# A step's x taken one step later in VectorE's order; the gate's moments on VectorE alone; the weights summed from x's place

## The chip, the cores and the metric

The kernel runs on one core of one Trainium2 chip. The metric is the device time of one execution in microseconds (us), as the median of timed runs. One more execution was taken with the hardware profiler on; the profile and the trace come from that one. The five engines of the core are called TensorE (PE in the profile; PEld is its weight load), VectorE (DVE), ScalarE (ACT), GpSimd (POOL) and SyncE (SP).

## The reference, cut to what matters

It is the forward pass of a recommender with attention over a user's history. The batch is B = 16,384, the history L = 200 items long, an embedding D = 64 numbers in float32, the item table 100,000 rows. In short:

```python
def dice(x, alpha, axis):
    mean = jnp.mean(x, axis=axis, keepdims=True)
    var = jnp.var(x, axis=axis, keepdims=True)
    p = jax.nn.sigmoid((x - mean) * jax.lax.rsqrt(var + EPS))
    return x * (p + alpha * (1.0 - p))

u, it, c = u_emb[user], i_emb[item], c_emb[cate]
h = i_emb[hist]                                   # [L, B, D]
itb = jnp.broadcast_to(it[None], h.shape)
feat = jnp.concatenate([h, itb, h - itb, h * itb], axis=-1)
a = dice(feat @ au_W1 + au_b1, au_alpha, axis=1)  # [L, B, 36]: moments over the batch
w = a @ au_W2 + au_b2                             # [L, B, 1]
cur = jnp.sum(w * h, axis=0)                      # [B, D]
z = jnp.concatenate([u, it, c, cur], axis=-1)
z = dice(z @ W1 + b1, alpha1, axis=0)
z = dice(z @ W2 + b2, alpha2, axis=0)
return z @ W3 + b3
```

The expensive part is the attention: 200 x 16,384 rows are looked up, each goes through a layer of 36 outputs, and the gate of that layer needs mean and variance over the whole batch of one history place before it can be applied.

## The kernel before

**Setup.** The layer is split by linearity. What depends on h alone (h times the first and third block of au_W1) is put behind each row of the item table once, so that `table` in DRAM has 128 numbers a row: h, and its part of x. What depends on the item alone is stored as `xi`. What is left for each history place is the product of h * item with the fourth block (`blk_m`).

**Steps.** A step k handles one chunk of 2,048 batch rows (16 rows on each of 128 partitions) of one history place: l, c = divmod(k, 8), so that eight steps make a place and 1,600 steps the whole. Seven turns of a hardware loop hold 24 places each (192 steps); the last 32 places (256 steps, `K`) follow without a loop, with pieces of the head's first layer (`base_of_layer1`, through `next(work)`) between them. At every loop turn all engines meet. The order of the instructions on each engine is the order of the program text (`manual_schedule`). Step k works on several chunks at once:

- `fetch(k)`: POOL issues sixteen indirect gathers of 128 rows each (L212) from `table` into one of twelve landing buffers `land`; SP loads `xi` of the chunk into one of two `xit` buffers.
- `gates(k-10)`: on ACT, sigmoid with scale and bias (L404, two halves) from x, which lies in the second half of the landing buffer's rows, into `pg` in PSUM, and then the line with alpha and the second layer's weight (L409). The scale and bias of a place are known only when its eight chunks have been through `hidden`, hence the distance of ten steps.
- `hidden(k-2)`: VectorE adds the product in PSUM (`px`) and the turned x part (`hx[:, 1]`), writes x into the landing buffer (L396), and takes batch statistics of both halves (L398).
- ACT copies `xit` into `px` (L482), onto which the product is accumulated.
- `turn(k-1)`: VectorE transposes h (L389) into `ph`, multiplies with the item (L390), and transposes the x part (L391). L389 is the first to need the gathered rows.
- `gated(k-10)`: VectorE multiplies gate and x (L415).
- `first_layer(k-1)`: TensorE's product, four matmuls of 128 x 512 in float32, each recorded as two (L243).
- `weigh(k-10)`: VectorE transposes the gated values (L420) into `hx[:, 0]`, sums 64 numbers for each row (L422), multiplies the row h with that weight (L427, scalar_tensor_tensor of `r` and `land`, both in SBUF), and adds to `cur` (L431).

`px` has two buffers that take turns in the loop; in the last 256 steps only the first is used for it, since the second (`pz`) takes the head's pieces.

**The end of a place.** In the step in which `hidden` handles the eighth chunk (`ends`), `bn_aggr` gives mean and variance of each partition (L438); the four groups of 32 partitions have to be averaged. That goes over TensorE: a matmul with the constant matrix `mean_of[S]` for the mean (L442), squares of deviations on VectorE (L447 to L449), a second matmul for the variance (L450), Sqrt on ACT (L452, with a table load[...]), and reciprocal and shift on VectorE (L458, L459). These pieces are laid between `turn`, `gated`, `first_layer` and `weigh`.

Of the kernel before, what the change touches and what calls it, by code (L numbers as in the profile page):

```python
# [14 lines left out]
P = 128  # L15
D = 64
# [5 lines left out]
LAND = 12  # L22
EARLY = 4
# [5 lines left out]
def din_kernel(  # L29
# [86 lines left out]
    for a in range(P // S):  # L116
# [19 lines left out]
    rstds = [const.tile([P, 2], F32, name=f"rs{i}") for i in range(2)]  # L136
    shifts = [const.tile([P, 2], F32, name=f"sh{i}") for i in range(2)]
# [27 lines left out]
        n: const.tile([n * m, n * m], F32, name=f"mean{n}") for n, m in ((ZA, 2), (ZB, 2 * J), (Z2, 2), (S, P // S))  # L165
# [182 lines left out]
    with ExitStack() as main:  # L348
# [20 lines left out]
        for i in range(2):  # L369
            nc.vector.memset(rstds[i], 0.0)  # L370
            nc.vector.memset(shifts[i], 0.0)
        nc.sync.dma_start(xit[-1 % XI], xi[ND - 1])

# [3 lines left out]
        def x_of(k):  # L377
            return land[k % LAND][:, :, D:]

# [13 lines left out]
        def hidden(k, px):  # L393

            l, c = divmod(k, ND)
            nc.vector.tensor_add(x_of(k), by_row(px), by_row(hx[k % 2][:, 1]))  # L396
            for q in range(2):
                nc.vector.bn_stats(stats[l % 2][:, q, c, :], x_of(k)[:, ts(q, TD // 2)])  # L398

        def gates(k):  # L400

            i = k // ND % 2
            for q in range(2):
                nc.scalar.activation(  # L404
                    by_row(pg)[:, ts(q, TD // 2)], x_of(k)[:, ts(q, TD // 2)], AF.Sigmoid,
                    bias=shifts[i][:, q : q + 1], scale=rstds[i][:, q : q + 1],
                )
# [6 lines left out]
        def gated(k):  # L414
            nc.vector.tensor_mul(by_row(pg), by_row(pg), x_of(k))  # L415

        def weigh(k):

            yT = hx[k % 2][:, 0]
            nc.vector.transpose(yT, pg)  # L420
            r = small.tile([P, TD], F32, tag="r", name="r")
            nc.vector.tensor_reduce(  # L422
                r, halves(yT).rearrange("p q n u -> p n q u"), mybir.AxisListType.XY, ALU.add
# [9 lines left out]
        mean, var = ph[:, 0:2], ph[:, 8:10]  # L433

        def moments_by_row(l):
# [3 lines left out]
            return mv  # L439

        def mean_of_groups(mv):
            nc.tensor.matmul(mean, mean_of[S], mv[:, :, 0], start=True, stop=True)  # L442

        def var_of_groups(mv):

            dev = small.tile([P, 2], F32, tag="dev", name="dev")
            nc.vector.tensor_sub(dev, mv[:, :, 0], mean)  # L447
            nc.vector.tensor_mul(dev, dev, dev)
            nc.vector.tensor_add(dev, dev, mv[:, :, 1])  # L449
            nc.tensor.matmul(var, mean_of[S], dev, start=True, stop=True)  # L450
            std = small.tile([P, 2], F32, tag="std2", name="std2")
            nc.scalar.activation(std, var, AF.Sqrt, bias=eps)  # L452
            return std

        def factors(l, std):

            i = l % 2
            nc.vector.reciprocal(rstds[i], std)  # L458
            nc.vector.scalar_tensor_tensor(shifts[i], mean, -1.0, rstds[i], ALU.mult, ALU.mult)  # L459

        def step(k, last=None):
# [4 lines left out]

            def px_of(j):

                return pxs[j % 2 if last is None or j < 0 else 0]

            l, c = divmod(k - 2, ND)
            ends = has(k - 2) and c == ND - 1
            if has(k):
                fetch(k)
            if has(k - 10):
                gates(k - 10)
            if has(k - 2):
                hidden(k - 2, px_of(k - 2))
            if ends:
                mv = moments_by_row(l)  # L480
            if has(k - 1):
                nc.scalar.copy(px_of(k - 1), xit[(k - 1) % XI])  # L482
                turn(k - 1)
            if ends:
                mean_of_groups(mv)
            if has(k - 10):
                gated(k - 10)
            if ends:
# [208 lines left out]
```

## Time and profile before

| | |
|---|---|
| timed runs (3) | 32,810.53 us median, 32,810.52 to 32,812.21 |
| the profiled execution | 36,985.32 us |
| its span, first to last instruction | 36,983.5 us |
| mean granted TensorE clock in it | 0.618 |
| busy in the span | PE 27%, PEld 11%, DVE 54%, ACT 19%, POOL 68% |
| gathers from `table` | 25,600, busy 24,929.8 us, 974 ns in the mean, 945 ns in the median |
| first and last gather start | 606.1 us, 36,780.7 us |
| VectorE's idle time before L396 | 15,628.3 us |
| VectorE's idle time before L389 | 478.4 us |
| DMA | 73 GB/s in the mean, 2,682 MB |

How to read the groups of the profile: line, engine, operation, output<-inputs by the program's names, shapes and count; then after the first bar busy time in us and the mean length of one in ns; after the second bar the idle time of the engine just before these instructions, and what ended most of it. "remote" and "issue" are waits for which the profile names no instruction. The ends of matmuls are modelled, so a wait for TensorE is read at the engine that waits. A line of the timeline holds start and length in us, engine, line, operation, names, shape and count, and in brackets the idle time before it and its releaser.

The profiled execution is 4.2 ms longer than the timed ones.

### The profile page before, as it was taken

What the parts mean: (1) busy time and instruction counts of PE and PEld (TensorE: products, weight loads), DVE (VectorE), ACT (ScalarE), POOL (GpSimd) and SP (SyncE); (2) the same over time, 40 slices, a digit from 0 to 9 for tenths busy, and PEclk for the clock granted to TensorE, in tenths of its full rate; (3) what the DMA queues carried; (4) which work ended last, traced back from release to release, by engine and by line L of the source; (5) the groups of instructions that cost most, each with busy time, mean ns of one, the idle gap of its engine ahead of it and who ended that gap; (6) DMA issues with size and microseconds to landing.
All of it is one profiled execution on the core that took longest, in us unless ns stands there. A gap on an engine that the chain in (4) does not pass through costs nothing. (4 is left out here: it accounts for less than half of the span.)

```text
span 36983.5 us, 116856 instructions
## 1 busy us (share of the span) xinstructions
PE 10134.8 (27%) x14456; PEld 4044.4 (11%) x14456; DVE 20049.6 (54%) x19476; ACT 7101.7 (19%) x8732; POOL 25299.4 (68%) x25992
## 2 busy tenths in 40 slices
PE   4222222222222222222222222222222222322223
PEld 1111111111111111111111111111111111111111
DVE  4555555555555555555555555555555555555555
ACT  0111211121111111111111111111111111211122
POOL 6766676676667666666766676676666676666665
PEclk7666666666666666666666666666666666666666
DMA  4222222222222222222222222222222222222222
GB/s 142 70 70 69 72 70 70 68 73 70 69 70 72 70 70 70 70 70 70 71 70 70 71 70 69 70 72 70 70 69 70 71 70 74 82 80 76 69 70 61
DMA packets 1219253, 2682.27 MB, mean 73 GB/s; under 512 B 552540, under 2 KB 578684, under 8 KB 1212284
## 3 DMA queue, kind: packets, MB, share of 16 engines
q0 software_dynamic: 831488, 1691.97, 17.4%
q1 hardware_dynamic: 375228, 914.56, 8.1%
q10 hardware_dynamic: 11712, 67.98, 0.5%
q14 instruction: 702, 5.75, 0.1%
q8 instruction: 123, 2.02, 0.0%
HBM read 2599.36 MB, written 73.35 MB: 72 GB/s over the span
## 5 line engine op out<-in xcount | busy, mean ns | idle before, releaser
L212 POOL DMA_INDIRECT land<-table,idx x25600 | 24929.8, 974 | 11288.1 <-issue 11053.1
L243 PE MATMUL px<-hx,blk_m 128*128 128x512 f32 x12824 | 9461.7, 906 | 22646.0 <-DVE hx L390 15979.1
L396 DVE TENSOR_TENSOR land<-px,hx 128x1024 f32<-128x1024 f32 x1602 | 1959.1, 1223 | 15628.3 <-remote 13918.8
L404 ACT ACTIVATE pg<-land,sh,rs 128x512 f32<-128x512 f32 x3220 | 2515.7, 781 | 23511.4 <-issue 21445.8
L243 PEld LDWEIGHTS px<-hx,blk_m 128*128 128x128 f32 x12824 | 3683.8, 302 | 28262.8 <-issue 27321.7
L409 ACT ACTIVATE pg<-pg,au_al,au_1al 128x512 f32<-128x512 f32 x3220 | 2419.0, 751 | 106.9
L389 DVE STREAM_TRANSPOSE ph<-land 128x1024 f32<-128x1024 f32 x1601 | 1992.7, 1245 | 478.4 <-DMA land<-table,idx 474.6
L427 DVE SCALAR_TENSOR_TENSOR pg<-r,au_bias,land 128x1024 f32<-128x1024 f32 x1610 | 2084.3, 1295 | 56.7
L398 DVE BATCH_NORM_STATS2 st<-land 128x6 f32<-128x512 f32 x3204 | 2061.2, 685 | 55.1
L420 DVE STREAM_TRANSPOSE hx<-pg 128x1024 f32<-128x1024 f32 x1610 | 2009.5, 1248 | 48.9
L482 ACT COPY px<-xit 128x1024 f32<-128x1024 f32 x1601 | 1613.1, 1008 | 2124.1 <-issue 1385.9
L431 DVE TENSOR_TENSOR cur<-pg,cur 128x1024 f32<-128x1024 f32 x1610 | 1970.6, 1224 | 54.9
L422 DVE TENSOR_REDUCE r<-hx 128x16 f32<-128x1024 f32 x1610 | 1964.0, 1220 | 55.3
L390 DVE TENSOR_TENSOR hx<-ph,itT 128x1024 f32<-128x1024 f32 x1601 | 1959.5, 1224 | 54.7
L391 DVE STREAM_TRANSPOSE hx<-land 128x1024 f32<-128x1024 f32 x1601 | 1974.6, 1233 | 0.0
L415 DVE TENSOR_TENSOR pg<-pg,land 128x1024 f32<-128x1024 f32 x1610 | 1930.8, 1199 | 5.4 <-ACT pg L409 5.3
L442 PE MATMUL ph<-mv,mean 128*128 128x2 f32 x402 | 117.9, 363 | 3346.9 <-issue 1834.8
L452 ACT ACTIVATE std<-ph,eps 128x2 f32<-128x2 f32 x201 | 52.7, 262 | 2829.2 <-remote 2360.5
L442 PEld LDWEIGHTS ph<-mv,mean 128*128 128x128 f32 x402 | 100.6, 311 | 3518.0 <-issue 1928.2
L404 ACT ACT_TABLE_LOAD x209 | 268.1, 1283 | 932.9 <-DMA table<-tab 338.0
L243 PE MATMUL px<-rT,blk_h 128*128 128x512 f32 (+1 forms) x392 | 236.1, 764 | 237.6 <-DVE rT L294 124.7
L452 ACT ACT_TABLE_LOAD x201 | 257.9, 1283 | 3.5
(109 smaller groups left out, 1711.6 us busy)
## 6 DMA issues: line engine op xcount, KB each, us to landing
xit<-xi SPq DMA_DIRECT2D x1601, 512.0 KB
land<-table,idx POOLq DMA_INDIRECT x25600
table<-tab ACTq DMA_DIRECT2D x48, 1024.0 KB
tab<-in_L_rec_i_emb SPq DMA_DIRECT2D x48, 512.0 KB
zt<-uicT SPq DMA_DIRECT2D x48, 512.0 KB
idx<-in_r_hist SPq DMA_DIRECT2D x200, 64.0 KB
uicT<-t ACTq DMA_DIRECT2D x24, 512.0 KB
zbase<-zt SPq DMA_DIRECT2D x10, 512.0 KB
```

The costliest lines, as they stand in the source:

```text
L212: nc.gpsimd.indirect_dma_start(out=dst[:, n, :], out_offset=None, in_=rows, in_offset=bass.IndirectOffsetOnAxis(ap=ids[:, n : n + 1], axis=0),
L243: nc.tensor.matmul(dst[:, q * CH : q * CH + n], blk[:, e, q], rhs[:, e * CH : e * CH + n], start=(e == 0 and not onto), stop=(e == 1), ski ...
L389: nc.vector.transpose(halves(ph), of_rows(rows[:, :, :D]))
L390: nc.vector.tensor_mul(hm, ph, itT[:, k % ND])
L391: nc.vector.transpose(halves(hw), of_rows(rows[:, :, D:]))
L398: nc.vector.bn_stats(stats[l % 2][:, q, c, :], x_of(k)[:, ts(q, TD // 2)])
L404: nc.scalar.activation(by_row(pg)[:, ts(q, TD // 2)], x_of(k)[:, ts(q, TD // 2)], AF.Sigmoid, bias=shifts[i][:, q : q + 1], scale=rstds[i] ...
L409: nc.scalar.activation(pg[:, ts(q, CH)], pg[:, ts(q, CH)], AF.Identity, bias=au_al[:, q : q + 1], scale=au_1al[:, q : q + 1],)
L420: nc.vector.transpose(yT, pg)
L422: nc.vector.tensor_reduce(r, halves(yT).rearrange("p q n u -> p n q u"), mybir.AxisListType.XY, ALU.add)
L427: nc.vector.scalar_tensor_tensor(by_row(pg), r.unsqueeze(2).to_broadcast([P, TD, D]), au_bias2, rows, ALU.add, ALU.mult,)
L431: nc.vector.tensor_add(cur[:, ts(c, TD)], by_row(pg), cur[:, ts(c, TD)])
```

## The change

- In step k, `turn(k-1)` and its product come first, then the moments where a place has ended, then `gates(k-10)` and `weigh(k-10)`, then `hidden(k-2)`, and last the copy of `xit` for step k itself (`preload(k)`), so that the product of step k+1 finds it there. Only in the last 144 steps (`SPAN`), where `px` has one buffer, do copy and product come behind `hidden(k-2)`.
- `moments(l)` replaces the four pieces at the end of a place. It is called once, in the step after the eighth chunk's `hidden`, and brings the four groups together by copies between partitions and by sums on VectorE; ACT still takes the square root. Scale and bias lie together in `facs`, which is copied back to the other three groups. `mean_of[S]` is no longer made.
- `gated` becomes the first instruction of `weigh`. x is now kept in the landing buffer in the layout of the turned values; `weigh` transposes the gated values into x's place, and the sum runs over 64 numbers that lie next to each other.
- The head's pieces are called from step K - 143 on.

```diff
@@ -20,6 +20,7 @@
 CD = 2 * CH
 LPB = 24
 LAND = 12
+SPAN = 144
 EARLY = 4
 IDX = 2
 XI = 2
@@ -133,8 +134,8 @@
     stats = [
         const.tile([P, 2, ND, nc.vector.BN_STATS_DIM], F32, name=f"st{i}") for i in range(2)
     ]
-    rstds = [const.tile([P, 2], F32, name=f"rs{i}") for i in range(2)]
-    shifts = [const.tile([P, 2], F32, name=f"sh{i}") for i in range(2)]
+
+    facs = [const.tile([P, 2, 2], F32, name=f"fac{i}") for i in range(2)]
     pxs = [psum.tile([P, CD], F32, name=f"px{i}") for i in range(2)]
     px, pz = pxs
     ph = psum.tile([P, CD], F32, name="ph")
@@ -162,7 +163,7 @@
     bias3 = const.tile([S, ZO], F32, name="bias3")
 
     mean_of = {
-        n: const.tile([n * m, n * m], F32, name=f"mean{n}") for n, m in ((ZA, 2), (ZB, 2 * J), (Z2, 2), (S, P // S))
+        n: const.tile([n * m, n * m], F32, name=f"mean{n}") for n, m in ((ZA, 2), (ZB, 2 * J), (Z2, 2))
     }
     zstats = [
         const.tile([n, m, nc.vector.BN_STATS_DIM], F32, name=f"zst{i}")
@@ -367,15 +368,15 @@
             for c in range(ND):
                 nc.vector.bn_stats(stats[-1 % 2][:, q, c, :], hx[0][:, 0, :CH])
         for i in range(2):
-            nc.vector.memset(rstds[i], 0.0)
-            nc.vector.memset(shifts[i], 0.0)
+            nc.vector.memset(facs[i], 0.0)
         nc.sync.dma_start(xit[-1 % XI], xi[ND - 1])
+        nc.scalar.copy(pxs[-1 % 2], xit[-1 % XI])
 
         def by_row(t):
             return t.rearrange("p (n d) -> p n d", d=D)
 
         def x_of(k):
-            return land[k % LAND][:, :, D:]
+            return of_rows(land[k % LAND][:, :, D:])
 
         def fetch(k):
             l, c = divmod(k, ND)
@@ -393,17 +394,17 @@
         def hidden(k, px):
 
             l, c = divmod(k, ND)
-            nc.vector.tensor_add(x_of(k), by_row(px), by_row(hx[k % 2][:, 1]))
+            nc.vector.tensor_add(x_of(k), halves(px), halves(hx[k % 2][:, 1]))
             for q in range(2):
-                nc.vector.bn_stats(stats[l % 2][:, q, c, :], x_of(k)[:, ts(q, TD // 2)])
+                nc.vector.bn_stats(stats[l % 2][:, q, c, :], x_of(k)[:, q])
 
         def gates(k):
 
             i = k // ND % 2
             for q in range(2):
                 nc.scalar.activation(
-                    by_row(pg)[:, ts(q, TD // 2)], x_of(k)[:, ts(q, TD // 2)], AF.Sigmoid,
-                    bias=shifts[i][:, q : q + 1], scale=rstds[i][:, q : q + 1],
+                    halves(pg)[:, q], x_of(k)[:, q], AF.Sigmoid,
+                    bias=facs[i][:, 1, q : q + 1], scale=facs[i][:, 0, q : q + 1],
                 )
             for q in range(2):
                 nc.scalar.activation(
@@ -411,16 +412,13 @@
                     bias=au_al[:, q : q + 1], scale=au_1al[:, q : q + 1],
                 )
 
-        def gated(k):
-            nc.vector.tensor_mul(by_row(pg), by_row(pg), x_of(k))
-
         def weigh(k):
 
-            yT = hx[k % 2][:, 0]
-            nc.vector.transpose(yT, pg)
+            nc.vector.tensor_mul(halves(pg), halves(pg), x_of(k))
+            nc.vector.transpose(x_of(k), halves(pg))
             r = small.tile([P, TD], F32, tag="r", name="r")
             nc.vector.tensor_reduce(
-                r, halves(yT).rearrange("p q n u -> p n q u"), mybir.AxisListType.XY, ALU.add
+                r, land[k % LAND][:, :, D:], mybir.AxisListType.X, ALU.add
             )
             c = k % ND
             rows = land[k % LAND][:, :, :D]
@@ -430,33 +428,36 @@
             )
             nc.vector.tensor_add(cur[:, ts(c, TD)], by_row(pg), cur[:, ts(c, TD)])
 
-        mean, var = ph[:, 0:2], ph[:, 8:10]
-
-        def moments_by_row(l):
+        def moments(l):
+
+            n = P // S
             mv = small.tile([P, 2, 2], F32, tag="mv", name="mv")
             for q in range(2):
                 nc.vector.bn_aggr(mv[:, q], stats[l % 2][:, q].rearrange("p c s -> p (c s)"))
-            return mv
-
-        def mean_of_groups(mv):
-            nc.tensor.matmul(mean, mean_of[S], mv[:, :, 0], start=True, stop=True)
-
-        def var_of_groups(mv):
-
-            dev = small.tile([P, 2], F32, tag="dev", name="dev")
-            nc.vector.tensor_sub(dev, mv[:, :, 0], mean)
+            every = small.tile([S, n, 2, 2], F32, tag="every", name="every")
+            for a in range(n):
+                nc.vector.tensor_copy(every[:, a], mv[ts(a, S)])
+            means = every[:, :, :, 0]
+            mean = small.tile([S, 2], F32, tag="mean", name="mean")
+            nc.vector.tensor_reduce(
+                mean, means.rearrange("p a q -> p q a"), mybir.AxisListType.X, ALU.add
+            )
+            nc.vector.tensor_scalar_mul(mean, mean, -1.0 / n)
+            dev = small.tile([S, n, 2], F32, tag="dev", name="dev")
+            nc.vector.tensor_add(dev, means, mean.unsqueeze(1).to_broadcast([S, n, 2]))
             nc.vector.tensor_mul(dev, dev, dev)
-            nc.vector.tensor_add(dev, dev, mv[:, :, 1])
-            nc.tensor.matmul(var, mean_of[S], dev, start=True, stop=True)
-            std = small.tile([P, 2], F32, tag="std2", name="std2")
-            nc.scalar.activation(std, var, AF.Sqrt, bias=eps)
-            return std
-
-        def factors(l, std):
-
-            i = l % 2
-            nc.vector.reciprocal(rstds[i], std)
-            nc.vector.scalar_tensor_tensor(shifts[i], mean, -1.0, rstds[i], ALU.mult, ALU.mult)
+            nc.vector.tensor_add(dev, dev, every[:, :, :, 1])
+            var = small.tile([S, 2], F32, tag="var", name="var")
+            nc.vector.tensor_reduce(
+                var, dev.rearrange("p a q -> p q a"), mybir.AxisListType.X, ALU.add
+            )
+            std = small.tile([S, 2], F32, tag="std2", name="std2")
+            nc.scalar.activation(std, var, AF.Sqrt, bias=eps[:S], scale=1.0 / n)
+            fac = facs[l % 2]
+            nc.vector.reciprocal(fac[:S, 0], std)
+            nc.vector.tensor_mul(fac[:S, 1], mean, fac[:S, 0])
+            for a in range(1, n):
+                nc.vector.tensor_copy(fac[ts(a, S)], fac[:S])
 
         def step(k, last=None):
 
@@ -464,35 +465,37 @@
             def has(j):
                 return last is None or j <= last
 
+            def single(j):
+
+                return last is not None and j > last - SPAN
+
             def px_of(j):
-
-                return pxs[j % 2 if last is None or j < 0 else 0]
-
-            l, c = divmod(k - 2, ND)
-            ends = has(k - 2) and c == ND - 1
+                return pxs[0 if single(j) else j % 2]
+
+            def preload(j):
+                nc.scalar.copy(px_of(j), xit[j % XI])
+
+            def product(j):
+                first_layer(px_of(j), blk_m, hx[j % 2][:, 0], onto=True)
+
             if has(k):
                 fetch(k)
+            if has(k - 1):
+                turn(k - 1)
+                if not single(k - 1):
+                    product(k - 1)
             if has(k - 10):
+                if k % ND == 2:
+                    moments((k - 10) // ND)
                 gates(k - 10)
+                weigh(k - 10)
             if has(k - 2):
                 hidden(k - 2, px_of(k - 2))
-            if ends:
-                mv = moments_by_row(l)
-            if has(k - 1):
-                nc.scalar.copy(px_of(k - 1), xit[(k - 1) % XI])
-                turn(k - 1)
-            if ends:
-                mean_of_groups(mv)
-            if has(k - 10):
-                gated(k - 10)
-            if ends:
-                std = var_of_groups(mv)
-            if has(k - 1):
-                first_layer(px_of(k - 1), blk_m, hx[(k - 1) % 2][:, 0], onto=True)
-            if has(k - 10):
-                weigh(k - 10)
-            if ends:
-                factors(l, std)
+            if has(k - 1) and single(k - 1):
+                preload(k - 1)
+                product(k - 1)
+            if has(k) and not single(k):
+                preload(k)
 
         def fetch_ids(k, l0, n):
             l, c = divmod(k, ND)
@@ -601,7 +604,7 @@
             for k in range(K):
                 fetch_ids(k, L - rest_l, rest_l)
                 step(k, last=K - 1)
-                if k > 1:
+                if k > K - SPAN:
                     next(work, None)
             load_base(0, 1)
             for k in range(K, K + 10):

```

## The prediction

> **What bounds the kernel now.** I read four views in this order: the page's groups, who waited for whom, the timeline of one quiet step, and the timeline around a long gather. First two groups of the page with two more of VectorE's, then a line of the gathers' own view, then one of the waits:
>
> ```profile
> L212 POOL DMA_INDIRECT land<-table,idx x25600 | 24929.8, 974 | 11288.1 <-issue 11053.1
> L243 PE MATMUL px<-hx,blk_m 128*128 128x512 f32 x12824 | 9461.7, 906 | 22646.0 <-DVE hx L390 15979.1
> L396 DVE TENSOR_TENSOR land<-px,hx 128x1024 f32<-128x1024 f32 x1602 | 1959.1, 1223 | 15628.3 <-remote 13918.8
> L389 DVE STREAM_TRANSPOSE ph<-land 128x1024 f32<-128x1024 f32 x1601 | 1992.7, 1245 | 478.4 <-DMA land<-table,idx 474.6
> ...
> L212 POOL DMA_INDIRECT land<-table,idx x25600: 938/945/2163, 606.1 to 36780.7; - x199
> ...
> DVE land L396 <- remote: 13918.8, 1227, 21.2
> ```
>
> GpSimd (POOL) issues 25,600 gathers of 128 rows, sixteen to a step, 1,600 steps. The first begins at 606.1 us, the last ends at 36,781.7, and 201.8 us follow. In the profiled execution VectorE stands 15.6 ms ahead of L396 (`hidden`), which waits for TensorE. Taken alone, that line says TensorE bounds the kernel and the change goes to the right place. It has to be held against a step in which this wait does not occur (columns: start, length, engine, line; idle time in brackets):
>
> ```profile
> 6394.33 0.94 POOL L212 DMA_INDIRECT land<-table,idx  x1 [0.30 <-issue]
> 6394.48 1.26 DVE L389 STREAM_TRANSPOSE ph<-land 128x1024 f32<-128x1024 f32 x1 [7.60 <-DMA land<-table,idx]
> ...
> 6397.14 5.99 PE L243 MATMUL px<-hx,blk_m 128*128 128x512 f32 x8 [14.24 <-DVE hx L390]
> ...
> 6401.82 0.94 POOL L212 DMA_INDIRECT land<-table,idx  x1 [0.30 <-issue]
> 6401.84 1.29 DVE L427 SCALAR_TENSOR_TENSOR pg<-r,au_bias,land 128x1024 f32<-128x1024 f32 x1
> ...
> 6404.31 1.21 DVE L396 TENSOR_TENSOR land<-px,hx 128x1024 f32<-128x1024 f32 x1
> ...
> 6414.47 1.26 DVE L389 STREAM_TRANSPOSE ph<-land 128x1024 f32<-128x1024 f32 x1 [7.13 <-DMA land<-table,idx]
> ```
>
> Here L396 follows L431 at once, the idle time lies before L389, which waits for the rows to land, and the step takes 6414.47 - 6394.48 = 19.99 us: sixteen gathers at 0.94 + 0.30 us. 606.1 + 1600 x 19.99 + 201.8 = 32,792 us, and the median of the timed runs is 32,810.5. So the timed runs are this quiet step repeated 1,600 times, within 0.06%: POOL's issuing of gathers bounds them, and the wait at L396 has no room in them. It belongs to the profiled execution (36,985.32 us; span 36,983.5), 4.2 ms longer, where L396 starts 12 to 17 us after its product's first matmul although the matmuls are recorded as 5 to 7 us long. What slows TensorE there the trace does not tell; I take it not to act in the timed runs, because 2.6 (L389, L390) + 17.3 + 2.5 (L396, L398) = 22.4 us a step would make 36.6 ms.
>
> What can reach POOL? This pair shows it (the line of the gather from the timeline some 3 ms later):
>
> ```profile
> 9403.16 1.29 DVE L427 SCALAR_TENSOR_TENSOR pg<-r,au_bias,land 128x1024 f32<-128x1024 f32 x1
> 9403.56 1.70 POOL L212 DMA_INDIRECT land<-table,idx  x1 [0.30 <-issue]
> ```
>
> L427 begins 0.84 us after the gather of 9402.32, and the next gather, which begins while L427 runs, lasts 1.70 us instead of 0.94. Going through the L427 starts of the trace: one between about 0.09 and 1.15 us after a gather's start lengthens the next gather by that distance less 0.09 us, up to 1.05; one from 0.09 us before a start to 0.09 after it costs nothing. In quiet steps L427 starts from 0.065 us before to 0.081 us after a gather's start: free, with 0.02 us to spare at the early end.
>
> [...] L427 (r and land) is the one large VectorE instruction here with two SBUF inputs[...] The granted clock was 0.618 and the quiet product took 5.99 us, but it has 20 us[...]
>
> **The change part by part.**
>
> (1) `hidden(k-2)` goes behind `weigh(k-10)`, `preload` (L482's copy, 1.01 us on ACT) to the end of the step before. After L389 VectorE issues L390, L391, the multiply, transpose, reduce, L427, L431, then L396 and L398: the order of the quiet step. The same eleven instructions, about 12.3 us of 20. L396 gets a product one step older; no wait removed in the timed runs, 0 us. Cover: 7.1 to 7.6 us of idle before L389. The copy must wait for L396 in its own step (about 11.1 us after L389), ends by 12.3, and the gates behind it on ACT take 3.2, to 15.5; the multiply needs them at 20 + 3.6. SP's load of xit waits for the copy two steps earlier, which now comes 1 to 2 us sooner. POOL's landing slot of step k is freed by `weigh(k-12)` in step k-2, as before; that step ends before gather k-1 starts. POOL therefore waits for nothing new: 0.
>
> (2) `weigh` writes its transpose into land and reduces along one axis. What counts is whether L427 moves against the gathers. Rows: L415 1,199 ns, L420 1,248 ns, L422 1,220 ns. The new transpose goes from PSUM into land's strided half; the setup's transpose L301 has that pattern, and its full-size instructions take 1,249 ns at the median. Transposes of this size lie between 1,203 and 1,249 ns, two-input operations between 1,199 and 1,225: a shift of -46 to +26 ns. I take 0. At +26 nothing; at -46 some 9% of the quiet steps come earlier than the free 0.09 us, 0.09 x 1400 x 1.03 = 130 us.
>
> (3) Moments, once in eight steps, 200 times. Removed: two pairs of tiny matmuls and VectorE work within the step; in such a step L427 came at 6422.15, 7.68 us after L389 instead of 7.36, 0.34 us into a gather: 0.25 us each, 50 us in all. Added, now ahead of the gates, from L389: both bn_aggr 3.57 to 4.15; four copies 4.19 to 4.58 (setup's L115 starts 0.08 apart from its neighbours, 0.15 long); six dependent instructions at 0.185 (spacing of L447, L448, L449), to 5.70; Sqrt on ACT 0.26 with 0.1 of hand-over each way, 6.13 (its table load was early before, too); reciprocal, multiply, three copies, 6.81; 0.07 hand-over; table load and four activations 4.46 (36,803.61 to 36,808.07 in the tail), 11.34. The multiply starts at 11.37 instead of 3.59: 7.78 later. Behind it on VectorE stand `weigh` and `hidden`; the step needs 12.3 + 7.8 = 20.1 us against 19.99 plus POOL's own delay, so the next L389 is on time to 0.1 us and at most its L427 is late by as much, which is nearly free. L427 itself comes at 6401.84 + 7.78 = 6409.62, 0.31 us into the gather of 6409.31: 0.22 us, against 0.25 before. No row shows two of these instructions (the small reduces), and the chain of seventeen may be off by 0.4 us: 0 to 0.6 us each, and 1.05 if it is early by over 0.4. So -50 to +70 us for the 200 steps, of which I take the middle, +10; at the far end +160. The small copies and adds last 0.15 to 0.2 us each; L447 to L449 show no longer gathers, so 0.
>
> (4) The last 144 steps keep one px. There the product starts after `hidden`, at about 12.3, and is due at 29.8 after L389: 6 us in 17.5, nothing. Before, this held for all 256 steps of the last part; the base work (116 pieces) fits in the 143 steps that call it. Setup loses one small mean matrix: under 1 us on POOL before 606, where the table's stores decide.
>
> (5) Tail. Before, the factors of the last layer stood ready 20.1 us after the last L389 (36,783.40 to 36,803.54). Now, from the same L389: turn 3.6, `weigh` and `hidden` to 12.3, gates to 13.1, `weigh` to 19.3, `hidden` to 21.8, moments 3.2 (6.81 - 3.57): 25.0, so 5 us more. Behind the factors both kernels have the same eight gates and weighings.
>
> Sum: 0 + 0 + 10 + 0 + 5 = 15 on 32,810.5: 32,825. Against the profiled execution the sum is different: the wait at L396 goes because the product may take 27 us, so its span should fall from 36,983.5 by 3.4 to 4.1 ms, to some 32.9 to 33.6 ms (in the last 144 steps 17.3 us plus the base work's matmuls do not fit in 17.5). That drop would be no gain in the timed runs.
>
> **The rivals.**
>
> A, slower: L427 slips off its free place. For it: 0.02 us of margin, and three instructions between L389 and L427 whose patterns change. Against it: the nearest rows give no shift. The price is up to 1.05 us a step; it decides above 0.041 us a step on average (65.6 us in 1,600). With 10% of the steps hit (1600 x 0.1 x 1.03 = 165) or every moments step at 1.05 (+160), the time is about 32,980; with 40% hit, 660 more, 33,470.
>
> B, faster: the timed runs hold some of TensorE's wait after all, and POOL is quicker there than in the trace. For it: the trace shows the wait at L396 over 1,200 times. Against it: POOL's traced pace alone already makes 32,792. At that pace the most to gain is 32,810.5 - 606.1 - 201.8 - 1600 x 19.97 = 51 us, 32,760; only a pace quicker by 1% untraced would let it reach 32,490.
>
> C, the moments' stall on VectorE runs over and holds up POOL. The price is nothing until VectorE lags two steps (40 us); 7.6 us of idle in each other step take it up. Time as forecast.
>
> **How the numbers follow.** No change, with parts 3 and 5 as small as worked out (C included): 0.60, 32,750 to 32,900. A: 0.32. B: 0.08. A measurement tells about 0.2%, 65.6 us, from no change. Of the first case 0.05 lies above 32,876: slower 0.37, same 0.55, faster 0.08. The range of 8 in 10 runs from 32,750 (no delay in the moments step) to 33,050 (the -46 ns shift and a bad place of the moments step: 130 + 110).
>
> **What would show it.** In the changed kernel's profile L396 should start right behind L431, the idle time should lie before L389 with the landing as its releaser, and quiet steps should stay at 19.97 to 20.0 us. L427 should stand within 0.09 us of a gather's start, and 7.8 us later in the step with the moments. If POOL's gathers have grown beyond 974 ns on average, A has happened. If the time falls by more than 51 us, POOL's pace in timed runs is not the traced one, and the reading of the bound is wrong.

## The result and the profile after

The changed kernel takes 32,925.49 us (median of 7 runs, 32,922.55 to 32,926.78), the kernel before 32,811.33 (7 runs, 32,810.43 to 32,812.22): ratio 1.0035, 95% interval 1.0023 to 1.0046. It is slower by 114 us, 0.35%. That lies inside the forecast range of 32,750 to 33,050, but 100 us above the predicted 32,825 and on the side forecast as second in chance. The profiled execution took 32,925.16 us, its span is 32,922.9.

The groups of the profile after (line, engine, operation, tiles; busy us and mean ns; idle time before and its releaser):

```profile
L213 POOL DMA_INDIRECT land<-table,idx x25600 | 24348.1, 951 | 7875.1 <-issue 7674.0
...
L390 DVE STREAM_TRANSPOSE ph<-land 128x1024 f32<-128x1024 f32 x1601 | 2016.5, 1259 | 10697.6 <-DMA land<-table,idx 10590.4
...
L425 DVE SCALAR_TENSOR_TENSOR pg<-r,au_bias,land 128x1024 f32<-128x1024 f32 x1610 | 2085.1, 1295 | 56.7
...
L397 DVE TENSOR_TENSOR land<-px,hx 128x1024 f32<-128x1024 f32 x1602 | 1945.1, 1214 | 0.0
```

L397 (before: L396, with 15,628.3 us of idle time ahead of it) waits for nothing. VectorE's idle time now lies ahead of L390 (before: L389) and ends with the landing of rows. An ordinary step, from the timeline:

```profile
6418.34 1.26 DVE L390 STREAM_TRANSPOSE ph<-land 128x1024 f32<-128x1024 f32 x1 [7.56 <-DMA land<-table,idx]
...
6421.00 6.70 PE L244 MATMUL px<-hx,blk_m 128*128 128x512 f32 x8 [13.51 <-DVE hx L391]
...
6425.66 0.94 POOL L213 DMA_INDIRECT land<-table,idx  x1 [0.30 <-issue]
6425.70 1.29 DVE L425 SCALAR_TENSOR_TENSOR pg<-r,au_bias,land 128x1024 f32<-128x1024 f32 x1
6426.91 0.94 POOL L213 DMA_INDIRECT land<-table,idx  x1 [0.31 <-issue]
...
6438.33 1.26 DVE L390 STREAM_TRANSPOSE ph<-land 128x1024 f32<-128x1024 f32 x1 [7.62 <-DMA land<-table,idx]
```

It takes 6438.33 - 6418.34 = 19.99 us, as before. L425 (before: L427) starts 0.04 us after a gather's start, and the gather behind it keeps its 0.94 us. Now a step with the moments, which comes once in eight (k%8 = 2):

```profile
6980.54 1.26 DVE L390 STREAM_TRANSPOSE ph<-land 128x1024 f32<-128x1024 f32 x1 [7.65 <-DMA land<-table,idx]
...
6984.73 0.84 DVE L439 COPY every<-mv 32x4 f32<-32x4 f32 x4
...
6985.60 0.15 DVE L442 TENSOR_REDUCE mean<-every 32x2 f32<-32x8 f32 x1
...
6986.73 0.29 ACT L455 ACTIVATE std<-var,eps 32x2 f32<-32x2 f32 x1 [12.81 <-DVE var L451]
...
6987.43 0.51 DVE L460 COPY fac<-fac 32x4 f32<-32x4 f32 x3
...
6995.35 0.94 POOL L213 DMA_INDIRECT land<-table,idx  x1 [0.30 <-issue]
6996.30 1.29 DVE L425 SCALAR_TENSOR_TENSOR pg<-r,au_bias,land 128x1024 f32<-128x1024 f32 x1
6996.60 1.81 POOL L213 DMA_INDIRECT land<-table,idx  x1 [0.30 <-issue]
...
7001.34 1.26 DVE L390 STREAM_TRANSPOSE ph<-land 128x1024 f32<-128x1024 f32 x1
```

L425 starts 6996.30 - 6980.54 = 15.76 us after L390 and 0.95 us into a gather, and the next gather lasts 1.81 us instead of 0.94. In the trace this holds for nearly all of these steps: in nine of ten L425 stands 0.92 to 0.96 us into a gather, 192 of 200 have a gather longer than 1.0 us, and POOL takes 20.80 us for the step in the mean, against a median of 19.97 for the others. The whole trace has 255 gathers longer than 1.0 us, 191.8 us in all above 0.944, and every one of them begins while an L425 runs.

### The profile page after: what moved, and what is told of

It reads as the page before. It is cut to its first block, busy times and chain, and to the rows that moved or that the text cites. A ratio compares the mean times of both kernels' runs of the same rounds, so it can differ in the third digit from the quotient of the medians.

```text
span 32922.9 us, 106947 instructions
## 1 busy us (share of the span) xinstructions
PE 9897.1 (30%) x13650; PEld 3847.8 (12%) x13650; DVE 20486.1 (62%) x21482; ACT 7127.0 (22%) x8732; POOL 24717.0 (75%) x25991
## 5 line engine op out<-in xcount | busy, mean ns | idle before, releaser
L213 POOL DMA_INDIRECT land<-table,idx x25600 | 24348.1, 951 | 7875.1 <-issue 7674.0
L390 DVE STREAM_TRANSPOSE ph<-land 128x1024 f32<-128x1024 f32 x1601 | 2016.5, 1259 | 10697.6 <-DMA land<-table,idx 10590.4
L405 ACT ACTIVATE pg<-land,fac 128x512 f32<-128x512 f32 x3220 | 2508.9, 779 | 85.8 <-DVE cur L429 25.0
L425 DVE SCALAR_TENSOR_TENSOR pg<-r,au_bias,land 128x1024 f32<-128x1024 f32 x1610 | 2085.1, 1295 | 56.7
L418 DVE STREAM_TRANSPOSE land<-pg 128x1024 f32<-128x1024 f32 x1610 | 2011.7, 1250 | 55.4
L420 DVE TENSOR_REDUCE r<-land 128x16 f32<-128x1024 f32 x1610 | 1964.0, 1220 | 55.3
L397 DVE TENSOR_TENSOR land<-px,hx 128x1024 f32<-128x1024 f32 x1602 | 1945.1, 1214 | 0.0
L439 DVE COPY every<-mv 32x4 f32<-32x4 f32 x804 | 161.7, 201 | 15.2
L213 POOL DMA_INDIRECT land<-in_L_rec_i_emb,ids x128 | 126.4, 987 | 41.0 <-issue 38.6
```

Source lines behind the costliest of these rows:

```text
L213: nc.gpsimd.indirect_dma_start(out=dst[:, n, :], out_offset=None, in_=rows, in_offset=bass.IndirectOffsetOnAxis(ap=ids[:, n : n + 1], axis=0),
L390: nc.vector.transpose(halves(ph), of_rows(rows[:, :, :D]))
L397: nc.vector.tensor_add(x_of(k), halves(px), halves(hx[k % 2][:, 1]))
L405: nc.scalar.activation(halves(pg)[:, q], x_of(k)[:, q], AF.Sigmoid, bias=facs[i][:, 1, q : q + 1], scale=facs[i][:, 0, q : q + 1],)
L418: nc.vector.transpose(x_of(k), halves(pg))
L420: nc.vector.tensor_reduce(r, land[k % LAND][:, :, D:], mybir.AxisListType.X, ALU.add)
```

## The experiments

Theory T, the collision: the time lost is the gathers that L425 lengthens, chiefly in the moments steps. The trace shows the lengthening, 1.81 us for 0.94; that it hangs on L425's having both r and rows in SBUF was an assumption of the author's, which the first two runs put to the test. The rivals: O, VectorE's longer moments step as such is passed on to POOL, wherever L425 stands; S, the small copies and sums of the moments hold up POOL themselves; P, the new order or its tail costs the time. The letters appear so in what is quoted. The runs came in four groups, each on one chip; ratios are against the kernel before in the same group, which took 32,815.76, 36,912.01, 36,927.6 and 32,816.41 us.

### Take L425's collision away, with every instruction kept

In the changed kernel (r goes to PSUM, to columns of ph that are free there):

```diff
-            r = small.tile([P, TD], F32, tag="r", name="r")
+            r = ph[:, CH : CH + TD]
```

> The changed kernel with one edit: the sums r of weigh lie in PSUM (a free bank of ph) instead of SBUF, so that the scalar_tensor_tensor has one input in SBUF and not two. Theory T (in the step with the moments this instruction starts 0.95 us into a gather and holds up the next gather by 0.82 us, 200 times): the hold-up goes, 32,925 - 165 = about 32,760 us, and about 32,740 if the few collisions of the other steps go too; no gather is long in that step any more, while the step on VectorE stays 8.4 us later than usual. Rival O (VectorE's work in that step, 20.75 us against 19.97 us, is what paces POOL): 32,925. Rival S (the small copies and sums of the moments hold up POOL): 32,925.

32,730.53 us (32,729.27 to 32,731.47), against 32,815.76 of the kernel before: ratio 0.9974 (0.9964 to 0.9984).

```profile
L213 POOL DMA_INDIRECT land<-table,idx x25600 | 24153.5, 943 | 7875.4 <-issue 7721.1
...
L425 DVE SCALAR_TENSOR_TENSOR pg<-ph,au_bias,land 128x1024 f32<-128x1024 f32 x1610 | 2081.6, 1293 | 57.2
```

L425 lasts as long (1,293 ns for 1,295) and so does VectorE's work; the gathers' busy time falls by 24,348.1 - 24,153.5 = 194.6 us and the kernel's by 195.0 (against the changed kernel's 32,925.49, from the first runs, in which the kernel before took 4 us less). In the moments steps L425 still starts 0.95 us into a gather, and the longest gather is now 0.96 us instead of 1.98. That is T, and O, S and P are out as main causes, since all that they blame is still there. What holds a gather up while L425 reads r from SBUF no run shows. The same edit in the kernel before:

> The kernel before with the same edit: r in PSUM. Theory T: it loses only what the scalar_tensor_tensor cost there, 0.25 us in each of 200 steps that end a place, and stray collisions: 32,811 - 50 = about 32,760 us. If the collision is not what costs time: 32,811.

32,725.57 us (32,723.6 to 32,726.99): ratio 0.9972 (0.9962 to 0.9983). Its rows for the gathers and for VectorE's two places of waiting:

```profile
L212 POOL DMA_INDIRECT land<-table,idx x25600 | 24153.2, 943 | 7877.6 <-issue 7674.9
...
L389 DVE STREAM_TRANSPOSE ph<-land 128x1024 f32<-128x1024 f32 x1601 | 2016.3, 1259 | 11587.3 <-DMA land<-table,idx 11587.3
...
L396 DVE TENSOR_TENSOR land<-px,hx 128x1024 f32<-128x1024 f32 x1602 | 1949.2, 1217 | 339.9 <-PE px L243 223.8
```

In the old order, too, VectorE waits for rows here and hardly for TensorE: 340 us ahead of L396, where the profile before has 15,628.

So the kernel before held 32,815.76 - 32,725.57 = 90 us of collisions, more than the 50 expected. Freed of them, the two kernels differ by 5 us: the whole change, its collisions apart, costs 5 us, and the collisions 195 - 90 = 105. Together 110, of 114 measured. This is also the fastest kernel of the study, 90 us below the kernel before; the change has no part in that.

### Move the moments

Put behind `hidden` in the step before (k%8 = 1), ahead of the preload:

```diff
             if has(k - 10):
-                if k % ND == 2:
-                    moments((k - 10) // ND)
                 gates(k - 10)
...
                 hidden(k - 2, px_of(k - 2))
+                if k % ND == 1:
+                    moments((k - 9) // ND)
```

> The changed kernel with the moments called at the end of the step before, behind hidden of the eighth chunk, in VectorE's idle time, with r in SBUF as in the changed kernel. Theory T: the scalar_tensor_tensor of every step starts 7.37 us after L390, free of a gather's start: about 32,760 us. Rival O: the same, since no step is longer than 16 us. Rival S (the small copies and sums themselves hold up POOL): 32,925, wherever they stand. Rival P (the new order or its tail costs the 114 us): 32,925.

32,872.67 us (32,868.84 to 32,876.96): ratio 1.0017 (1.0011 to 1.0024). It wins 53 us of the 165 expected. L425 is back at 7.37 us after L390 in every step, but in the steps k%8 = 2 it mostly still stands 0.50 to 0.94 us into a gather. A timeline of one such step:

```profile
6965.70 0.29 ACT L455 ACTIVATE std<-var,eps 32x2 f32<-32x2 f32 x1 [18.37 <-DVE var L451]
6965.90 1.00 ACT L476 COPY px<-xit 128x1024 f32<-128x1024 f32 x1
...
6966.92 0.32 SPq L384 DMA_DIRECT2D xit<-xi  x1
...
6971.34 1.26 DVE L390 STREAM_TRANSPOSE ph<-land 128x1024 f32<-128x1024 f32 x1 [4.43 <-DMA land<-table,idx]
...
6978.70 1.29 DVE L425 SCALAR_TENSOR_TENSOR pg<-r,au_bias,land 128x1024 f32<-128x1024 f32 x1
6979.32 1.49 POOL L213 DMA_INDIRECT land<-table,idx  x1 [0.30 <-issue]
```

The preload's copy now stands behind Sqrt on ScalarE, so SP's load of xit, which waits for the copy, goes out 6.3 us after L397's start, some 4 us later than in other steps, close to the landing of the step's last rows. L390 then starts 2.35 us (median) after the last gather's end instead of 1.70, and L425 with it. In the next variant the moments stand behind the loads, at the end of step k%8 = 1:

```diff
             if has(k) and not single(k):
                 preload(k)
+            if has(k - 2) and k % ND == 1:
+                moments((k - 9) // ND)
```

It was first run in a group at 36.9 ms, where it could not tell (below), and then with half of TensorE's product left out, which is read beside the changed kernel with that alone:

```diff
-        for q in range(2):
+        for q in range(half):
             for e in range(2):
...
-                first_layer(px_of(j), blk_m, hx[j % 2][:, 0], onto=True)
+                first_layer(px_of(j), blk_m, hx[j % 2][:, 0], onto=True, half=1)
```

> The changed kernel with half of TensorE's product in the main loop (the four matmuls of the second half of px are left out, so x is wrong there). On a chip where TensorE sets the time (the kernel before takes 36.9 ms): if a product is paced by its own work, 22.40 us becomes about 11.2 us, less than the 19.97 us of 16 gathers, and the kernel is bound by the gathers again, 32,925 us with 200 long steps (32,850 to 33,000); if what holds it is a wait of fixed length on the release, 36,690 us again. On a chip where the kernel before takes 32.81 ms: 32,925 us, since TensorE is not on the path.

32,925.32 us (32,922.14 to 32,929.75): ratio 1.0034 (1.0021 to 1.0046), in a group where the kernel before takes 32,816.41. It is the changed kernel's own time: TensorE is not on the path there.

> Half of the product left out, and the moments at the end of step k%8=1, behind the loads. Collision, with the late load of xit as what spoilt the place ahead of the preload: no moments step has long gathers, the half product's own time - 165 us, 32,760 us. If the moments hold the gathers wherever they stand: 32,870 us. If the half product stays at 36,690: 36,675.

32,756.46 us (32,752.03 to 32,760.16): ratio 0.9982 (0.9975 to 0.9989), 168.9 us less than with the moments in their place. L390 comes 1.70 us after the last gather again, L425 stands 0.03 us into a gather (median) in the steps k%8 = 2 as in the others, and 6 of these 200 steps have a gather longer than 1.0 us, where the changed kernel with the half product has 193:

```profile
L213 POOL DMA_INDIRECT land<-table,idx x25600 | 24180.3, 945 | 7874.8 <-issue 7659.7
```

So the moments as such, the same seventeen small instructions on VectorE, cost nothing; where they push L425 costs 168.9 / 200 = 0.84 us each. That it was the late load that delayed the landing in the variant before is argued from the timeline: the two places differ in more than that load.

### Push L425 on, and pull it back

One aggregation issued a second time in the moments step:

```diff
                 nc.vector.bn_aggr(mv[:, q], stats[l % 2][:, q].rearrange("p c s -> p (c s)"))
+            nc.vector.bn_aggr(mv[:, 1], stats[l % 2][:, 1].rearrange("p c s -> p (c s)"))
```

> The changed kernel with one bn_aggr of the moments issued twice (same result), about 0.28 us more on VectorE. Theory T: in the moments step the scalar_tensor_tensor then starts within 0.03 us of a gather's start, which is free, so POOL is not held up in that step, but VectorE is 1.06 us late for the next landing, and the instruction of the next step starts 1.08 us into a gather and holds up the next one by 0.99: 32,925 + 200 x (0.99 - 0.82) = about 32,960 us, with the long gathers moved from the moments step to the one after it. If lateness does not carry over: 32,760. Rival O: 0.28 us more for each of 200: 32,981, with the long gather in the same step as before. Rival S: about 32,925.

32,947.95 us (32,944.57 to 32,948.57): ratio 1.0040 (1.0026 to 1.0054). L425 of the moments step now starts 16.13 us after L390 and 0.05 us into the next gather: no long gather follows it. VectorE is then late for the step after, whose L425 stands 1.09 us into a gather, and the long gather is there, 1.94 us, which is 1.00 more than usual. The loss moved with L425, not with the moments.

The other way, less work: the sum for r over 48 of 64 numbers, which leaves out a quarter of each sum. It was run twice in groups at 36.9 ms (below), and then with half of the product left out as above:

```diff
-                r, land[k % LAND][:, :, D:], mybir.AxisListType.X, ALU.add
+                r, land[k % LAND][:, :, D : D + 48], mybir.AxisListType.X, ALU.add
```

> Half of the product left out, and the sum for r over 48 of 64 numbers (a quarter of each sum is left out): the test of the collision that the runs on a TensorE-bound chip could not make, since 0.27 us less work now comes where the gathers bind. Collision: ordinary steps' scalar_tensor_tensor from 0.02 us into a gather to about 1.0 us into the one before, +0.9 us each, moments steps 0.2 us less: the half product's own time + 1,210 us, 34,130 us (33,700 to 34,300). If VectorE's length is what costs: the half product's time or up to 55 us less. If the half product stays at 36,690: 36,690.

34,104.04 us (34,101.16 to 34,106.97): ratio 1.0392 (1.0375 to 1.0409).

```profile
L213 POOL DMA_INDIRECT land<-table,idx x25600 | 25534.0, 997 | 7874.6 <-issue 7803.2
...
L425 DVE SCALAR_TENSOR_TENSOR pg<-r,au_bias,land 128x1024 f32<-128x1024 f32 x1610 | 2083.7, 1294 | 57.2
...
L420 DVE TENSOR_REDUCE r<-land 128x16 f32<-128x768 f32 x1610 | 1534.2, 953 | 55.3
```

The sum is 267 ns shorter, VectorE has 430 us less to do, and the kernel is 1,179 us slower: L425 of the ordinary steps (median) has moved from 0.03 us into a gather to 1.01 us into the one before it, 0.9 us a step. No theory of VectorE's length gives a loss here. For the opposite, L425 some 0.34 us later in every step, there is no time.

The gathers' busy time accounts for all these times. Time is the median of the timed runs, busy time that of the profiled execution, both in us, and the rest is their difference; it stays within 10 us while the times spread over 1.4 ms:

| kernel | time | gathers busy | the rest |
|---|---|---|---|
| before, r in PSUM | 32,725.57 | 24,153.2 | 8,572.4 |
| changed, r in PSUM | 32,730.53 | 24,153.5 | 8,577.0 |
| moments last (half product) | 32,756.46 | 24,180.3 | 8,576.2 |
| moments early | 32,872.67 | 24,294.9 | 8,577.8 |
| changed | 32,925.49 | 24,348.1 | 8,577.4 |
| changed (half product) | 32,925.32 | 24,348.1 | 8,577.2 |
| one more aggregation | 32,947.95 | 24,368.6 | 8,579.4 |
| shorter sum (half product) | 34,104.04 | 25,534.0 | 8,570.0 |

The 26.8 us between the second and third row are about what the ordinary steps lose to L425 in the changed kernel. In each of these traces with r in SBUF, every gather longer than 1.0 us begins while an L425 runs; with r in PSUM none is longer than that.

### The groups at 36.9 ms

In two groups of runs the kernel before takes 36,912.01 us (17 runs, 36,879.85 to 36,930.57) and 36,927.6 (7 runs). The expectations take this for a property of the chip. That is not shown: the record has chip number 6 for the first of these groups and 4 for the second, and 4 also for the first experiments above, at 32,815.76 us; whether one number is one and the same chip it does not say. It may be a state that lasts through a group. The kernel before, profiled there:

> The kernel before, unchanged, profiled once more. If the wait of L396 on TensorE (15.6 ms in the profile of before) belongs to this kernel's order, its span is again near 36,980 us; if it belonged to that one execution, the span is near 32,810 us, the products' releases come 5 to 7 us after their start, and the starts of its scalar_tensor_tensor within the gathers account for some 90 us of longer gathers, which is what taking r out of SBUF won. Time 32,811 to 32,816 us either way.

36,898.85 us (12 runs), span 36,909.6, with the wait of the profile that the prediction was made from:

```profile
L396 DVE TENSOR_TENSOR land<-px,hx 128x1024 f32<-128x1024 f32 x1602 | 1960.0, 1223 | 15240.1 <-remote 13262.4
```

```profile
18759.24 1.22 DVE L396 TENSOR_TENSOR land<-px,hx 128x1024 f32<-128x1024 f32 x1 [10.04 <-remote]
18761.70 1.24 DVE L389 STREAM_TRANSPOSE ph<-land 128x1024 f32<-128x1024 f32 x1
18764.35 6.27 PE L243 MATMUL px<-hx,blk_m 128*128 128x512 f32 x8 [16.88 <-DVE hx L390]
18781.64 1.22 DVE L396 TENSOR_TENSOR land<-px,hx 128x1024 f32<-128x1024 f32 x1 [10.03 <-remote]
```

The second fence is its timeline: 22.40 us from one L396 to the next, with the product recorded as 6.27 us long. Neither answer of the expectation held: the wait does not come with this kernel everywhere (340 us ahead of L396 with r in PSUM, above), nor was it one execution's, since here the timed runs have it too. The changed kernel, in the other of the two groups:

> The changed kernel, unchanged. On a chip where the kernel before takes 32.81 ms: 32,925 us, ratio 1.0035, 200 long steps of 20.8 us. On a chip where the kernel before takes 36.9 ms and TensorE's products end one per 22.40 us: 36,680 us, ratio 0.9936, as the variant with the moments last had there, since the place of the moments on VectorE lies beside the wait on TensorE; a ratio over 1.0 there would say that the variant's place of the moments, and not the order, won its 0.64%.

36,690.26 us (36,685.08 to 36,706.42): ratio 0.9938 (0.9921 to 0.9954), faster by 0.62%. Here the change gains 237 us, about twice what it loses where the kernel before takes 32.8 ms. Its waits, from the profile's rows:

```profile
L213 POOL DMA_INDIRECT land<-table,idx x25600 | 27048.5, 1057 | 8834.1 <-issue 8609.7
...
L390 DVE STREAM_TRANSPOSE ph<-land 128x1024 f32<-128x1024 f32 x1601 | 2014.3, 1258 | 12194.4 <-DMA land<-table,idx 10801.1
L397 DVE TENSOR_TENSOR land<-px,hx 128x1024 f32<-128x1024 f32 x1602 | 1944.7, 1214 | 1763.7 <-remote 1454.8
```

The wait is 1,764 us at L397 where it was 15,240 at L396, yet the span is only 36,909.6 - 36,682.8 = 227 us shorter (the two traces are of the two groups). The trace of before has products starting every 22.58 us in the mean of the hardware loop, that of after every 22.39; the release of a product comes 17.2 us (median) after its first matmul before, and 19.9 us after. The product with more time took more. Counted by POOL's gathers, the steps k%8 = 3 took 26.9 us in the mean before and 22.6 after, 860 us for 200 of them; the other seven of eight took 21.6 to 22.4 before and 22.1 to 23.2 after, which gives back some 630 us. Three more runs in these groups come out within 20 us of the changed kernel, whatever was done to the moments or the sum:

> The changed kernel with the moments at the very end of step k%8=1, behind the loads of the next step, so that no SyncE load and no preload copy stands behind ScalarE's Sqrt. The weights' scalar_tensor_tensor of step k%8=2 should then sit 7.37 us after its turn like all others, and the turn should come 1.70 us after the last gather's start again, not 2.35 us. Collision, with the late load as what spoilt the former place of the moments: no long gathers, 32,925 - 165 = 32,760 us. If the moments themselves (their own reads of SBUF) are what held the gathers there: 32,870 us again. If a place of the moments is worth nothing: 32,925 us.

36,672.92 us, ratio 0.9936 (0.9923 to 0.9950).

> The changed kernel with less work: the sum for r runs over 48 of 64 numbers (a quarter of each sum is left out), so that the scalar_tensor_tensor starts about 0.27 us earlier in every step. Collision: ordinary steps' start moves from 0.02 us into a gather to about 1.0 us into the one before it, 0.9 us longer each, 1,400 x 0.9 = +1,260 us; moments steps from 0.95 to 0.68, 0.23 us shorter, -46 us; together 34,130 us (33,700 to 34,300). If VectorE's length is what costs: 32,925 us or less, 32,870 with 0.27 us off each moments step.

36,678.04 us, ratio 0.9937 (0.9924 to 0.9951). The same kernel in the second of these groups:

> The changed kernel with the sum for r over 48 of 64 numbers (a quarter of each sum is left out), so that the scalar_tensor_tensor starts about 0.27 us earlier in every step; on a chip where the kernel before takes 32.81 ms. Collision: ordinary steps' start moves from 0.02 us into a gather to about 1.0 us into the one before it, 0.9 us longer each, 1,400 x 0.9 = +1,260 us; moments steps from 0.95 to 0.68, -46 us; together 34,130 us (33,700 to 34,300), although there is less work. If VectorE's length is what costs: 32,870 to 32,925 us. Where the kernel before takes 36.9 ms: 36,680 us, as in the run on such a chip, and nothing is told apart.

36,686.25 us, ratio 0.9936 (0.9919 to 0.9952).

Why TensorE's products come slowly in these groups stays open. The half product was meant to test whether they are paced by their own work, but its group was one at 32.8 ms. The way in which the pace reaches POOL in the changed kernel stays open too. The time shows up there as longer gathers (1,057 ns in the mean), but L425 is not the main reason: 9,337 gathers are longer than 1.0 us, 2,849 us in all above 0.944, and those that overlap an L425 hold 921 us of it.

## Why the prediction was right in part

**The bound** was read rightly: the wait at L396 has no room in the timed runs of 32.81 ms, POOL's gathers set the time, and rival B, with TensorE's wait in those runs, is out (with r in PSUM the kernel before waits 340 us ahead of L396, and in the changed kernel the half product changed nothing). But that the sum of 32,792 us came out so close was luck. It took the setup from the profiled execution, 606.1 us to the first gather; in the traces at 32.7 to 32.9 ms it is 488.6 to 488.9. The 117 us too many were more than made up by what the sum left out: 90 us of collisions, and six long steps at the turns of the hardware loop (27.1 us for the first, 30.4 for the others, 59 us together above a quiet step).

**Part (1)**, the order: right, no cost. Quiet steps stayed at 19.97 to 19.99 us, and with the collisions away all of the change costs 5 us.

**Part (2)**, the layout of the weighing: right. L425 stands 0.02 us into a gather in the median of the ordinary steps; the shift of -46 ns did not come. The price set on such a shift was real: 0.27 us earlier cost 1,179 us.

**Part (3)**, the moments, is the term that failed, in its size. It placed L427 at 15.14 us after L389, 0.31 us into a gather, for 0.22 us each, and took +10 us of a span of -50 to +70. It came at 15.76 in the step shown (15.79 in the median), 0.95 us in, for 0.84 us each. The chain's working, held against the step shown above: the aggregations end at 4.2 us, as forecast. The four copies last 0.84 us together and the next instruction starts at 5.06 after L390, where 4.58 was forecast: they had been set 0.08 us apart, from a setup row, and stand 0.17 apart, the first 0.34 from the second. The three copies at the end (L460), priced the same way, are 0.2 us longer than thought; Sqrt's hand-over is 0.07 shorter. Table load (1.28 us of it) and activations take 4.46 us, as forecast. 0.48 + 0.20 - 0.07 = 0.61 us of the 0.62. The working had allowed for an error of 0.4 us, and its rule for what a start within a gather costs was right: 0.95 - 0.09 = 0.86 us, 0.84 found. In the other half of the term, the kernel before held 90 us of collisions, not the 50 read from a trace whose steps were of another length. Its trace with r in PSUM shows L427 in the step that ends a place 0.42 us into a gather, not 0.34, and VectorE late into the step after, whose L427 stands 0.61 us in; that second step had been put at nothing. By the prediction's rule this makes 0.33 us each for the first and, less that delay, 0.19 for the second: an estimate of 104 us. Altogether 200 x 0.84 + 27 - 90 = 105 us, in place of +10.

**Part (4)**, the last 144 steps: right; from step 1,456 to the end of the last gather both kernels with r in PSUM take 2,875.7 us. **Part (5)**, the tail: 8 us (210.2 against 202.4), 5 forecast.

**Rival A** is the mechanism that happened, in the form named there as every moments step at 1.05 us. The sign set for it did not show it: the gathers' mean did not grow beyond 974 ns, it is 951. That mark came from the profile before, in which only 631 of the 2,398 gathers longer than 1.0 us overlap an L427. The kernel before has 943 ns with r in PSUM, and some 947 with its 90 us of collisions (an estimate). **Rival C** was right to cost nothing, but had less margin than thought: in the moments step shown VectorE is through 20.77 us after L390 begins, and the next L390 follows 0.03 us later.

**The profiled span** was forecast at 32.9 to 33.6 ms, and 32.92 was found, for the wrong reason: the profile after was taken where the products are released 5.9 us (median) after their first matmul. Where they are slow, the span fell by 227 us, not by 3.4 to 4.1 ms. The step that failed is "because the product may take 27 us": it took the 17.3 us for the length of a product, which more time would cover. With more time the release came later, after 19.9 us for 17.2, and the products still started 22.4 us apart.

## What to carry to other kernels

Where an engine that issues DMAs sets the time and a second engine's instruction can hold up an issue (here 1.81 us for 0.94), an edit's price can be the place of that instruction within the issue's period and not the length of the work added: here 0.27 us less work in a step cost 3.6%, and moving one small operand to PSUM was worth more (195 us) than any place of the moments (168.9). A forecast that depends on a phase of 0.1 us can't be made from a chain of seventeen instructions priced to 0.4 us; take the whole period as the range. Where the operand can be moved so that the two no longer collide, the phase stops mattering: with r in PSUM the two kernels differ by 5 us. And compare the span of a profile with the timed runs before reading waits in it; if they differ by 10%, find out first which of the two the change will be measured on.

## What had not been expected of the hardware

The same kernel takes 32.81 ms in some groups of runs and 36.91 in others, at a granted clock of 0.617 to 0.619 in the latter's profiles against 0.633 in those with r in PSUM. The clocks lie 2 to 3% apart, the releases much further: products recorded as 5.9 us long (median) are released after 17.2, and where the kernel takes 32.7 to 32.9 ms, recorded as equally long, after 5.8 to 5.9. In the timeline of the kernel before in these groups one L396 follows the other after 22.40 us; in the profile before, 36.98 ms, the commonest distance between the releases of successive products is 22.5 us. What sets these distances no run shows. And a DMA load issued some 4 us late, close to where gathered rows land, went with a landing that VectorE saw 0.65 us later.
